# Two products of V and two of the next keys by turns, in place of four and four, in a cross-attention kernel on one core

## The chip, the core and the metric

The kernel runs on one NeuronCore of a Trainium2 chip. Its engines work side by side, each through its own instructions in order, and wait for one another by semaphores: TensorE (PE in the profile; PEld are its weight loads) multiplies matrices into PSUM, VectorE (DVE) and ScalarE (ACT) take results out of PSUM and compute on SBUF, GpSimd (POOL) computes on SBUF alone, and SyncE (SP) issues most DMAs. The metric is the device time of one execution in microseconds (us), as the median of several runs.

## What is computed

A cross attention in float32, for 16 batches of 100 queries of width 640, 8 heads of width 80, over 718 context rows of width 384. The last 4 of the 722 rows take a way of their own, whose result is added before the output projection. Cut to what matters:

```python
query = hidden_states @ Wq
keyt = enc @ Wk                       # enc: the first 718 rows, 384 wide
valt = enc @ Wv
hs = _mha(query, keyt, valt)          # 8 heads: softmax(q k^T / sqrt(80)) v
ca_hs1 = _mha(ca_q1, residual, residual)
ca_q2 = ca_hs1 @ Wq
ca_hs2 = _mha(ca_q2, ca @ Wk_ca, ca @ Wv_ca)   # ca: the last 4 rows
out = (hs + ca_hs2) @ Wout + b_out + residual
```

## The kernel before

One loop runs over the 16 batches (`b`, line 1218), with the order of every engine's instructions written out by hand: each engine takes its instructions in the order in which the program makes them. Each batch goes through the same stages. `scores` (three calls, L622) multiplies queries with keys for three pairs of key blocks and ScalarE copies the scores to the tiles `st[0]` to `st[2]`. VectorE takes the maximum (`larger`, L1252; the class `Maximum`). Then, while the maximum is being worked out, TensorE makes two things in small products: the values V of this batch (`vv`, class `Values`) and the keys of the next batch (`kk`, class `Keys`). After them come `last_keys` (L567), in some batches an output projection (`project_pair`, L1033) or the next queries (`queries`, L543), and at last the products of the exponentials with V (`a_ps`, L1432).

V and the keys are each made by a scheme of 15 products of sums of blocks, in place of 18 plain ones. `V_PLAN` lists for each product a PSUM bank (A to E), the form of the context and of the weights that it takes, and the block of the result into which the bank's content goes next. A bank isn't cleared between products: it goes on adding up, and after every product its content as it stands is taken out and added to one block (`Blocks.go`). So a product in a bank must wait until the content after the bank's previous product has been taken out. The first thing that reaches a block is a copy on ScalarE (L415), every later one an addition on VectorE (L413). `K_PLAN` is the same list for the keys, with two pairs of places exchanged.

In what follows v0 to v14 are the products of V in the order of `V_PLAN`, and k0 to k14 those of the keys in the order of `K_PLAN`. The banks that matter are:

| products | bank | block | taken out by |
|---|---|---|---|
| v3, k3 | A | (2, 0) | VectorE |
| v4, k4 | B | (2, 0) | VectorE |
| v5 | E (two PSUM buffers) | (1, 0) | VectorE, two additions |
| v6 | A | (1, 0) | VectorE |
| k5 | A | (1, 0) | VectorE |
| k6 | E | (1, 0) | VectorE |
| v7, k7 | B | (2, 1) | VectorE |
| v8, k10 | C | (0, 1) | ScalarE for v8, VectorE for k10 |
| v10, k12 | C | (2, 1) | VectorE |

A and B of V lie in a pair of banks each, A and B of the keys in a pool of two buffers (`psk`). C, D and E of both share one pool of two buffers (`ps1`) by turns: D of V takes both, then D of the keys one, then E of V both, E of the keys one, C of V both, C of the keys one. A product of V is two matmuls (two key blocks, L442) and one of the keys two (two chunks of the width, L473); the profile has two records for each matmul.

The function `both(n)` issues the next n products of V and then the next n of the keys, each with its removal. It is called in batches 1 to 14 (line 1311). Around the call that the change touches stand, in order: `top.go(3)`, `both(3)`, `now.scores2()`, `top.go(1)` (ScalarE spreads the maximum), `last.place()` (twenty small copies on ScalarE, L948), the touched call, `top.go()` (VectorE transposes the spread maximum into `over`, L704), `both(1)`, `now.softmax3()` (three small VectorE instructions, of which the last makes `p2`, L861), `now.values2()` (GpSimd's products and sums from `p2`, L875 and L882), two products of V and one of the keys, and then `subtract(0)` (L1240, VectorE takes `over` from the scores) and `exponential(0)` (ScalarE, L1248). The subtracts of the other two score tiles stand between the later products. In batches 3, 6, 8, 11 and 13 `last.load` has GpSimd add the bias to two tiles (L915) before `values2`, and the output of two blocks of rows is projected after `last_keys`.

Of the kernel before, what the change touches and what calls it, by code (L numbers as in the profile page):

```python
# [135 lines left out]
def kernel(  # L136
# [80 lines left out]
    def enc_tile(name):  # L217

        return inp.tile([P, NF, KT], F32, tag="enc", name=name)
# [14 lines left out]
    def load_rest(b, enc):  # L234
        if b == 1:
            room = hsT_tile("rest_1").rearrange("p c s -> p (c s)")
            rest = room[:, : len(A_REST) * KT].rearrange("p (i k) -> p i k", k=KT)
        else:
            rest = rest_tile(f"rest_{b}")
        for (u, c), i in A_REST.items():  # L240
            nc.sync.dma_start(
                out=rest[:, i], in_=enct[b][:, c, u * (KT - 1) : u * (KT - 1) + KT]
            )
        return enc[0], rest
# [347 lines left out]
    def last_keys(b, enc):  # L592
        banks = pair(f"kT_ps_{b}")
        return chunk_keys(
            HC - 1,
            [banks[:, k] for k in range(2)],
            [wk4[:, c] for c in range(CC)],
            enc,
        )
# [106 lines left out]
    def load_m(b):  # L706
        if b < 2:
            return lambda c: m_sb[c][:, b * HT : (b + 1) * HT]
        mb = small.tile([P, HC, HT], F32, tag="mb", name=f"mb_{b}", bufs=2)
        nc.sync.dma_start(  # L710
            out=mb, in_=m_d[:, :, b * HT : (b + 1) * HT].rearrange("c p n -> p c n")
        )
        return lambda c: mb[:, c]
# [504 lines left out]
    for b in range(B):  # L1218
# [5 lines left out]
        def loads():  # L1224

            if b == 0:
                nc.sync.dma_start(
                    out=wout_sb, in_=wout.rearrange("(c p) n -> p c n", p=P)
                )
            if b + 2 >= B:  # L1230
                return None, None
            x_next = xT_at[0] if b % 2 else load_x(p + 1)
            xT_at[0] = x_next
            return Second(b + 2, x_next), load_enc(b + 2)
# [4 lines left out]
        def subtract(i):  # L1239
            return nc.vector.tensor_tensor(  # L1240
                st[i],
                st[i],
                top.over[:KN].unsqueeze(1).to_broadcast([KN, 2, ROWS]),
                ALU.subtract,
            )

        def exponential(i):
            nc.scalar.activation(st[i], st[i], AF.Exp, scale=SCALE)  # L1248
# [59 lines left out]
        elif b + 1 < B:  # L1308
            vv = Values(b, e_in)

            def both(n):
                vv.go(n)
                kk.go(n)

            forms = [wout_sb[:, 2 * i : 2 * i + 2, k * (H // 2) : (k + 1) * (H // 2)]
                     for i in range(2) for k in range(2)]
            if b == 2:
                for o, left, right in (
                    (forms[1], forms[1], forms[0]),
                    (wout2[:, 0], forms[3], forms[1]),  # L1320
                    (wout2[:, 1], forms[2], wout2[:, 0]),
                ):
                    nc.gpsimd.tensor_tensor(o, left, right, ALU.subtract)
            elif last.b - 1 in PAIRS:
                nc.gpsimd.tensor_tensor(wout2[:, 0], wout2[:, 0], forms[0], ALU.add)
            second.scores1(seen)
            if b == 1:
                now.load()
            last.load()
            top.go(3)  # L1330
            both(3)
            now.scores2()
            top.go(1)
            if b > 1:
                last.place()
            both(4)
            top.go()
            both(1)
            now.softmax3()
            if b == 1:  # L1340
                nc.gpsimd.tensor_tensor(last.hs[:S], last.hs[:S], last.hs2, ALU.add)
            now.values2()
            if last.b in PAIRS:
                last.sums()
            vv.go(2)
            kk.go(1)
            subtract(0)
            exponential(0)
            vv.go(1)
            subtract(1)  # L1350
            vv.go(1)
            kk.go(2)
            exponential(1)
            vv.go(1)
            kk.go(2)
            both(1)
            both(1)
            if b == 1:
                for f in list(wv_there):
                    nc.scalar.copy(wv_sb[:, W_AT[f]], wv_there.pop(f))  # L1360
            second.load()
            if b == 1:
                nc.gpsimd.dma_start(out=bias, in_=bout[0].partition_broadcast(P))
            second_next, enc_next = loads()
            if b + 2 < B:
                m_next = load_m(b + 2)
            subtract(2)
            exponential(2)
            last_keys(b + 1, enc)
            if b + 2 < B:  # L1370
                enc_next = load_rest(b + 2, enc_next)
            if b == 1:
                last.transpose()
            if last.b in PAIRS:
                second.softmax1(3)
                last.project_pair()
                if last.b == max(PAIRS):
                    nc.sync.dma_start(
                        out=forms[1],
                        in_=wout[: 2 * P, H // 2 :].rearrange("(c p) n -> p c n", p=P),  # L1380
                    )
            second.softmax1()
        else:
            room = enc_tile("spare").rearrange("p f k -> p (f k)")
            spare.extend(room[:, i * H : (i + 1) * H] for i in range(2))
            last.transpose()
            vv = Values(b, e_in)
            last.load()
            mine.load()
            top.go(3)  # L1390
            vv.go(3)
            last.project_few(len(OC) - 2)
            now.scores2()
            top.go(1)
            vv.go(2)
            top.go()
            vv.go(3)
            now.softmax3()
            now.values2()
            vv.go(2)  # L1400
            subtract(0)
            exponential(0)
            vv.go(5)
            for i in (1, 2):
                subtract(i)
                exponential(i)
            last.project()
# [105 lines left out]
```

## Time and profile before

| | us |
|---|---|
| runs shown (3) | 942.48, 942.58, 943.21 |
| median | 942.58 |
| the profiled execution | 943.54 |
| its span, first to last instruction | 941.8 |
| TensorE matmuls busy | 930.6 (99%) |
| VectorE busy | 698.5 (74%) |
| GpSimd busy | 674.1 (72%) |
| ScalarE busy | 434.6 (46%) |
| 352 records of products of V in bank A, mean of one | 0.435 |
| 360 records of products of keys in bank A, mean of one | 0.369 |

The span is that of the one execution that the profiler recorded. Matmuls are pipelined: the records overlap, and a busy TensorE isn't a TensorE without gaps, so gaps are looked for in the distance from start to start. A row of the order of time gives the start and the length of a group in us, the engine, the line, the operation, output and inputs, the shapes, how many instructions are merged and, in brackets, idle time before them with what ended it. Idle time on an engine other than the one that sets the end costs nothing by itself. Batch 2 begins near 158 us, batch 3 near 206.6 us; its products of V and keys run from 215.5 to 244.8 us.

### The profile page before, as it was taken

What the parts mean: (1) busy time and instruction counts of PE and PEld (TensorE: products, weight loads), DVE (VectorE), ACT (ScalarE), POOL (GpSimd) and SP (SyncE); (2) the same over time, 40 slices, a digit from 0 to 9 for tenths busy, and PEclk for the clock granted to TensorE, in tenths of its full rate; (3) what the DMA queues carried; (4) which work ended last, traced back from release to release, by engine and by line L of the source; (5) the groups of instructions that cost most, each with busy time, mean ns of one, the idle gap of its engine ahead of it and who ended that gap; (6) DMA issues with size and microseconds to landing.
All of it is one profiled execution on the core that took longest, in us unless ns stands there. A gap on an engine that the chain in (4) does not pass through costs nothing.

```text
span 941.8 us, 25879 instructions
## 1 busy us (share of the span) xinstructions
PE 930.6 (99%) x11130; PEld 785.7 (83%) x11130; DVE 698.5 (74%) x1111; ACT 434.6 (46%) x836; POOL 674.1 (72%) x615
## 2 busy tenths in 40 slices
PE   9999999999999999999999999999999999999998
PEld 6998879797797878888798887988879888797866
DVE  3859794989739797695967859579783898838884
ACT  1235443736336363462635526264651736416341
POOL 5757998688937778497784968747895588945714
PEclk9999999999999999999999999999999999999999
DMA  8822022040300304031030310205030050310201
GB/s 258 280 71 71 23 79 62 5 149 2 101 31 20 106 1 130 3 93 61 14 117 3 111 43 29 75 2 151 4 96 34 2 152 2 101 45 2 80 18 41
DMA packets 49673, 62.82 MB, mean 67 GB/s; under 512 B 14072, under 2 KB 38200, under 8 KB 49560
## 3 DMA queue, kind: packets, MB, share of 16 engines
q1 hardware_dynamic: 45512, 51.49, 17.8%
q0 software_dynamic: 3024, 8.53, 2.9%
q8 instruction: 87, 1.43, 0.6%
q10 hardware_dynamic: 1024, 1.15, 0.4%
q14 instruction: 26, 0.21, 0.1%
HBM read 55.59 MB, written 5.57 MB: 65 GB/s over the span
## 4 chain that ended last, share of the span: by engine, by line
PE 85%; DVE 12%; issue 2%; ACT 1%; DMA 0%; POOL 0%; ACTq 0%; DVEq 0%
PE a_ps L1432 12%; PE s_ps L622 11%; PE kT_ps L567 8%; PE v_psA L442 8%; PE q_ps L543 7%; PE v_psB L442 7%; PE k_psA L473 6%; PE o_ps L1033 5%; PE k_psB L473 5%; PE v_psC L442 3%; DVE vs L413 3%; DVE st L1240 2%; PE k_psC L473 2%; DVE most L1252 2%; PE v_ps L383 2%
## 5 line engine op out<-in xcount | busy, mean ns | idle before, releaser
L783 POOL TENSOR_TENSOR e<-ca,g 100x800 f32<-100x800 f32 x64 | 99.4, 1563 | 133.4 <-DVE most L1252 124.2
L875 POOL TENSOR_TENSOR hs<-vb,p 100x640 f32<-100x640 f32 x64 | 119.8, 1881 | 53.1 <-DVE p L861 24.1
L508 POOL TENSOR_TENSOR enc<-enc 128x240 f32<-128x240 f32 x135 | 104.9, 786 | 20.0 <-DMA enc<-in_enct 12.9
L1432 PEld LDWEIGHTS a_ps<-vs,st 120*36 120x36 f32 (+3 forms) x3072 | 109.2, 125 | 5.7 <-issue 5.6
L1432 PE MATMUL a_ps<-vs,st 120*36 120x81 f32 (+3 forms) x3072 | 112.2, 233 | 0.7 <-issue 0.7
L442 PE MATMUL v_psA<-wv_sb,enc 128*120 128x320 f32 x352 | 110.0, 435 | 0.3
L1240 DVE TENSOR_TENSOR st<-st,over 120x1600 f32<-120x1600 f32 x48 | 107.1, 2234 | 0.0
L882 POOL TENSOR_TENSOR hs<-hs,hs 100x640 f32<-100x640 f32 x48 | 100.6, 2096 | 3.8
L622 PE MATMUL s_ps<-qp,kT 32*120 32x100 f32 x3072 | 98.3, 263 | 0.0
L622 PEld LDWEIGHTS s_ps<-qp,kT 32*120 32x120 f32 x3072 | 95.5, 179 | 1.7 <-issue 0.2
L639 ACT COPY st<-s_ps 120x800 f32<-120x800 f32 x64 | 49.7, 829 | 101.5 <-PE s_ps L622 101.5
L790 POOL TENSOR_TENSOR e<-e,e 100x800 f32<-100x800 f32 x48 | 90.5, 1886 | 3.8
L442 PE MATMUL v_psB<-wv_sb,enc 128*120 128x320 f32 x296 | 91.8, 433 | 0.0
L473 PE MATMUL k_psA<-enc,wk_sb 128*128 128x240 f32 x360 | 88.7, 369 | 3.0 <-DVE kT L413 2.2
L1248 ACT ACTIVATE st<-st 120x1600 f32<-120x1600 f32 x48 | 73.8, 1538 | 27.6 <-DVE st L1240 27.4
L1252 DVE TENSOR_TENSOR most<-most,st 120x800 f32<-120x800 f32 x64 | 68.7, 1074 | 23.3 <-ACT st L633 22.2
L473 PEld LDWEIGHTS k_psA<-enc,wk_sb 128*128 128x128 f32 x360 | 67.1, 190 | 22.3 <-issue 4.3
L442 PEld LDWEIGHTS v_psA<-wv_sb,enc 128*120 128x120 f32 x352 | 62.8, 183 | 24.4 <-DVE vs L413 2.9
L473 PE MATMUL k_psB<-enc,wk_sb 128*128 128x240 f32 x300 | 73.1, 366 | 0.3 <-DVE sm L858 0.3
L442 PEld LDWEIGHTS v_psB<-wv_sb,enc 128*120 128x120 f32 x296 | 54.1, 183 | 21.9 <-DVE vs L413 0.4
L1444 DVE RECIPROCAL rs<-a_ps 100x4 f32<-100x4 f32 x32 | 5.8, 180 | 86.0 <-PE a_ps L1432 86.0
L543 PE MATMUL q_ps<-xT,wq_sb 128*128 128x200 f32 x400 | 69.1, 333 | 0.0
(167 smaller groups left out, 1851.8 us busy)
## 6 DMA issues: line engine op xcount, KB each, us to landing
vb<-va_d POOLq DMA_DIRECT2D x32, 250.0 KB, 3.6
vb<-va_d SPq DMA_DIRECT2D x32, 250.0 KB
enc<-in_enct SPq DMA_DIRECT2D x30, 240.0 KB
enc<-in_enct SPq DMA_DIRECT2D x15, 360.0 KB
xT<-in_xt SPq DMA_DIRECT2D x8, 500.0 KB
rest<-in_enct SPq DMA_DIRECT2D x31, 120.0 KB
xn<-in_x SPq DMA_DIRECT2D x11, 320.0 KB
out<-xn SPq DMA_DIRECT2D x11, 320.0 KB
```

Of the source, the lines that this page charges most:

```text
L442: nc.tensor.matmul(at[0][j][:KN, : H // 2], a_form(self.enc, f)[:, j * KN : (j + 1) * KN], wv_there.get(f, wv_sb[:, W_AT[f]]), start=first ...
L473: nc.tensor.matmul(at[:, i * KT : (i + 1) * KT], wk_sb[:, W_AT[f], i], a_form(self.enc, f), start=(first and i == 0), stop=last, skip_grou ...
L508: nc.gpsimd.tensor_tensor(out, left, right, op)
L543: nc.tensor.matmul(q_ps[:, : 2 * S].rearrange("p (j s) -> p j s", j=2), wq_sb[:, c, n * P : (n + 1) * P], xT[:, :, c, :], start=(c == 0), ...
L622: nc.tensor.matmul(s_ps[r][:n, 256 * a + lo : 256 * a + hi], kT[rows, c, u, j * KN : (j + 1) * KN], rhs, start=(a == 0 and c == 0), stop=( ...
L783: first = nc.gpsimd.tensor_tensor(to, self.ca[:, t, :].unsqueeze(1).to_broadcast([S, NH, S]), g[:, :, t].unsqueeze(2).to_broadcast([S, NH, ...
L790: nc.gpsimd.tensor_tensor(e, e, to, ALU.add)
L875: first = nc.gpsimd.tensor_tensor(to, self.vb[t][:S].rearrange("p (h d) -> p h d", h=NH), p2[:, :, t].unsqueeze(2).to_broadcast([S, NH, D] ...
L882: nc.gpsimd.tensor_tensor(sums, sums, to, ALU.add)
L1240: return nc.vector.tensor_tensor(st[i], st[i], top.over[:KN].unsqueeze(1).to_broadcast([KN, 2, ROWS]), ALU.subtract,)
L1252: most_now = nc.vector.tensor_tensor(most[:KN], most[:KN], st[i][:, u], ALU.max)
L1432: nc.tensor.matmul(a_v[lo:hi, h % 4], st[i // 2][: KEYS[i], i % 2, h * S + lo : h * S + hi], block(i, h // 4)[: KEYS[i], h % 4], start=(i ...
```

## The change

One call becomes two, in batches 1 to 14:

```diff
             if b > 1:
                 last.place()
-            both(4)
+            both(2)
+            both(2)
             top.go()
             both(1)
             now.softmax3()
```

Before, the products come as v3, v4, v5, v6, k3, k4, k5, k6; after, as v3, v4, k3, k4, v5, v6, k5, k6. Every removal moves with its product, so VectorE's order becomes v3, v4, k3, k4, v5 (two additions), v6, k5, k6. Nothing else is changed.

## The prediction

> **What bounds the kernel now.** I read the page first, then the instructions of TensorE and of VectorE in order of time in two batches, then the same spots of all fourteen batches that run the changed line. The page:
>
> ```profile
> PE 930.6 (99%) x11130; PEld 785.7 (83%) x11130; DVE 698.5 (74%) x1111; ACT 434.6 (46%) x836; POOL 674.1 (72%) x615
> ...
> PE 85%; DVE 12%; issue 2%; ACT 1%; DMA 0%; POOL 0%; ACTq 0%; DVEq 0%
> ```
>
> The second line is the chain of work that ended last: 85% lies on TensorE and 12% on VectorE. So TensorE's work sets the end, and what can be won are the spots where it waits for VectorE. The order of time in batch 3 shows them (columns: start, length, engine, line, operation, tiles, count, idle time before and what ended it). TensorE:
>
> ```profile
> 223.35 1.24 PE L442 MATMUL v_psE<-wv_sb,enc 128*120 128x320 f32 x4
> 224.67 1.34 PE L442 MATMUL v_psA<-wv_sb,enc 128*120 128x320 f32 x4
> 225.85 0.97 PE L473 MATMUL k_psA<-enc,wk_sb 128*128 128x240 f32 x4
> 226.66 0.97 PE L473 MATMUL k_psB<-enc,wk_sb 128*128 128x240 f32 x4
> 227.98 1.05 PE L473 MATMUL k_psA<-enc,wk_sb 128*128 128x240 f32 x4 [0.35 <-DVE kT L413]
> 228.86 0.97 PE L473 MATMUL k_psE<-enc,wk_sb 128*128 128x240 f32 x4
> 229.67 1.24 PE L442 MATMUL v_psB<-wv_sb,enc 128*120 128x320 f32 x4
> ```
>
> Lengths overlap, so I go by starts. Undisturbed, a key product takes 0.81 us from start to start (225.85 to 226.66) and one of V 1.08 (the start of batch 2 has 166.88, 167.98, 169.06). Against that, v6 (the second v_psA) starts 0.25 late and its successor 0.10 more (the array fills again), and k5 (the second k_psA) 0.51 late, its successor 0.08 more: 0.94 us lost. VectorE in the same stretch:
>
> ```profile
> 223.81 0.81 DVE L413 TENSOR_TENSOR vs<-v_psA,vs 120x640 f32<-120x640 f32 x1
> 224.72 0.82 DVE L413 TENSOR_TENSOR vs<-v_psB,vs 120x640 f32<-120x640 f32 x1
> 225.46 0.88 DVE L413 TENSOR_TENSOR vs<-v_psE,vs 120x320 f32<-120x320 f32 x2
> 226.44 0.82 DVE L413 TENSOR_TENSOR vs<-v_psA,vs 120x640 f32<-120x640 f32 x1
> 227.19 0.65 DVE L413 TENSOR_TENSOR kT<-k_psA,kT 128x480 f32<-128x480 f32 x1
> ...
> 230.45 1.00 DVE L704 STREAM_TRANSPOSE over<-spread 128x800 f32<-128x800 f32 x1
> ...
> 233.09 0.97 DVE L861 TENSOR_TENSOR p<-e,sm 100x32 f32<-100x32 f32 x1
> ```
>
> Product v6 goes into bank A again and needs v3 (223.81 to 224.62) taken out. k5 likewise needs k3 taken out, which ends at 227.84. Only k4 stands between k3 and k5, 0.81 us, while a product's tail, the hop to VectorE and an addition of 0.66 take over 1.1. So k5 waits at least 0.35 (0.27 and 0.08) in every batch.
>
> **The same reading in all batches.** Early wait, v6 and k5 together: batch 1 0.99, batch 3 0.94, batch 5 0.96, batch 11 0.69, batch 13 0.77, batch 14 0.66, and 0.35 in each of 2, 4, 6, 7, 8, 9, 10, 12. Sum 7.81 us. A later wait stands at k12, the second k_psC, for the removal of k10: 0.60 in batch 1, 0.34 in eight others (2, 4, 5, 7, 9, 10, 12, 14), none in 3, 6, 8, 11, 13.
>
> **The change part by part.** No instruction is added or removed; 14 times v5, v6 trade places with k3, k4, with their eight matmuls each and five of VectorE's nine removals. No DMA and no ScalarE or GpSimd instruction is in the moved stretch, so the queues of SP and POOL are passed by nothing; ScalarE keeps its order, since all removals here are additions on VectorE.
>
> Switching between V and keys: now once per batch in this stretch, after it three times. The rows show k_psE to v_psB in 0.81 and v_psB to k_psB in 1.08, the undisturbed times, so it costs 0.
>
> v6 after v3: between them now v4, k3, k4, v5 instead of v4, v5. In batch 3 v6 would start at 221.20 + 1.08 + 1.08 + 0.81 + 0.81 + 1.08 = 226.05, and v3 is out at 224.62: no wait. k5 after k3: between them k4, v5, v6, 2.96 us in place of 0.81. k5 would start at 227.13; VectorE takes out v3 to 224.62, v4 to 225.55, k3 to 226.11: no wait. So the early wait goes in all batches, 7.81 us.
>
> Does VectorE follow? Its order is then v3, v4, k3, k4, v5 (two), v6, k5, k6. With the rows' lengths (an addition into what the one before wrote starts 0.10 after its end, any other 0.08 before): k4 226.87, v5 227.66, v6 228.59, k5 229.15, k6 229.92, and the transpose `over` starts at 229.83 instead of 230.45, 0.62 earlier. VectorE had idled 0.47 and 0.15 there. In batches with only the 0.35 wait, the removal of k6 follows TensorE's k6 by 0.04 as now, so VectorE moves by 0.35 with it.
>
> New waits: v5 opens E's two banks when D's are copied, which ScalarE has done by 221.96 in batch 3. k6 opens one of them again and needs v5 out: 227.27 against its start at 227.94, room of 0.67. In batch 2 the room is 1.2. It costs 0 here.
>
> Where the stall goes. After `over` comes p2 (L861), with both inputs in SBUF. It takes 0.19 us in batches 2, 4, 5, 7, 9, 10, 12, 14, but 0.97 in batch 3, where it ends with GpSimd's addition:
>
> ```profile
> 230.95 3.05 POOL L915 TENSOR_TENSOR xn<-xn,bias 128x640 f32<-128x640 f32 x2
> ```
>
> The two additions run to 234.00, p2 to 234.05, and only then the first subtract starts. The same holds in 6, 8, 11, 13 (L915) and in 1 (L790 to 127.40). There VectorE may arrive earlier and gets on no earlier, because GpSimd's chain began before the changed stretch. What TensorE gains is kept only up to k12, whose room is its start less the end of k10's removal: 0.28, 0.34, 0.33, 0.29, 0.29 in batches 3, 6, 8, 11, 13. Less 0.06 for the hop to TensorE (191.12 to 191.18 in batch 2) and 0.10 for the restart, 0.13 + 0.18 + 0.17 + 0.13 + 0.13 = 0.74. Batch 1 has no room and keeps 0.
>
> The open batches move as a whole: 2, 4, 7, 9, 10, 12 keep 0.35 each, 2.10; 14 keeps 0.66. Batch 5 keeps its 0.96 and more: its second subtract came 0.11 behind GpSimd's next product (353.125 against 353.015) and was held 1 us. The product stands behind p2 and moves 0.62, the subtract stands behind TensorE's v10 and moves 0.96, so now it goes first and the 0.33 at k12 goes too: 1.29.
>
> Sum: 2.10 + 0.66 + 1.29 + 0.74 = 4.79 us, of which nothing is lost later: the last exponential is covered by last_keys, 3.65 us, and by the 2.3 us that a_ps spends on the first two score tiles (in batch 2 it ends at 198.87 and is first used near 201.9), so the next batch starts earlier as a whole. The profiled execution took 943.54 (span 941.8), so 938.8 for it; it lies 0.96 above the median, and from the median 942.58 the forecast is 937.8.
>
> What is priced from no row is who wins when VectorE and GpSimd come at once. With the 0.62, p2 of batch 3 is ready at 232.47 and GpSimd's second addition starts at 232.45; batches 1, 11, 13 are as close. Bounds: p2 second, as summed; p2 first with the subtract straight after it, which frees the whole early wait there, 0.99 + 0.81 + 0.56 + 0.64 = 3.0 more; p2 first and then the subtract behind the addition, 1.55, which puts it 0.25 later than now and takes back 0.4 in each of these four, 1.6 less. I take p2 second, since it is nearest to the rows (0.11 late lost in batch 5).
>
> The Trainium skill, page "SBUF — State Buffer", section "SBUF: two separate sides", says that VectorE with two SBUF inputs and GpSimd take a shared port as an exclusive lock for a whole instruction, first come first; that is what p2's two lengths show. By it alone the earlier VectorE would be worth nothing wherever GpSimd started 0.02 before it, the 4.8 above, and 7.8 if it started 0.02 after; the page doesn't say who goes first at a tie.
>
> **The rivals.**
> - Everything early is kept, because p2 gets in between GpSimd's two additions: 4.8 + 3.0 = 7.8, so 934.8. For it: the margins are hundredths. Against: at present p2 is late in all four. 21%.
> - VectorE takes it back: its subtracts don't move in the eight open batches either, and the wait at k12 grows by what went early. Then 0.74 and perhaps half of batch 5 stay, about 1.4: 941.2. For it: k12 waits for VectorE already there. Against: VectorE's idle 0.47 and 0.15 before k5's and k6's removals show that TensorE paced it. 14%.
> - Slower: the place is k6, which needs E's bank, emptied 1.3 us later than now. It decides once VectorE is later than the sum by 0.67 (batch 3) or 1.2 (batch 2); the price is one for one beyond that. With each of the six additions from v3 to v5 0.35 longer than its row, 2.1 in all, the wait would be 1.4 in the five batches like 3 and 0.9 in the nine like 2, 15.1, less the 7.81, so 949.9. Against: additions in this very place hold 0.81 and 0.66 with GpSimd busy beside them. 5%.
> - The change doesn't do what it says: k5 waits for something else than k3's removal (a form written by GpSimd is also waited for). Then no difference, 942.6. 3%.
>
> **How the numbers follow.** The forecast, 3.4 to 6 us less (936.6 to 939.2), has 57%. The range 934.4 to 939.8 takes in the first rival. This kernel's measurement tells about 0.2%, 1.9 us, from no change: faster 0.57 + 0.21 + 0.04 of the second rival = 0.82, same 0.10 + 0.03 = 0.13, slower 0.05.
>
> **What would show it.** v5 to v6 and v6 to k5 1.08 from start to start, with no idle before either, in all 14 batches: the mechanism. `over` 0.6 earlier in batch 3 relative to the batch's start: VectorE follows. p2 still ending with L915, and a new wait of some 0.7 at k12 in batch 3, 0.3 in 6 and 8: the taking back; p2 at 0.19 there: the first rival. No wait at k12 in batch 5. A wait at k6 would speak for the slower case, and a k12 wait that grows in batch 2 for the second rival.

## The result and the profile after

| | before | after |
|---|---|---|
| median, us | 942.53 (6 runs, 942.06 to 943.53) | 937.99 (6 runs, 936.77 to 939.92) |
| the profiled execution, us | 943.54 | 936.77 |
| its span, us | 941.8 | 935.1 |

The ratio is 0.9952, with a 95% interval of 0.9939 to 0.9966: 4.5 us less, by an interval that lies wholly below 1. The profiled execution of after is the fastest of its six, so the two profiles stand further apart, 6.8 us, than the medians.

The page after, first the busy times, then the chain of work that ended last, then TensorE's group in `a_ps`:

```profile
PE 926.5 (99%) x11130; PEld 786.6 (84%) x11130; DVE 699.4 (75%) x1111; ACT 434.6 (46%) x836; POOL 674.8 (72%) x615
...
PE 86%; DVE 11%; issue 1%; DMA 1%; ACT 1%; POOL 0%; DVEq 0%
...
L1433 PE MATMUL a_ps<-vs,st 120*36 120x81 f32 (+3 forms) x3072 | 112.0, 233 | 0.0
```

The work is the same. The share of VectorE in the chain fell by a point. The last line had 0.7 us of idle time in the profile before and has none now, though nothing of it was changed; this comes back below.

The order of time of TensorE in batch 3 after, in the stretch that was shown before (columns as there):

```profile
220.05 1.24 PE L442 MATMUL v_psB<-wv_sb,enc 128*120 128x320 f32 x4
221.12 0.97 PE L473 MATMUL k_psA<-enc,wk_sb 128*128 128x240 f32 x4
221.94 0.97 PE L473 MATMUL k_psB<-enc,wk_sb 128*128 128x240 f32 x4
222.75 1.24 PE L442 MATMUL v_psE<-wv_sb,enc 128*120 128x320 f32 x4
223.82 1.24 PE L442 MATMUL v_psA<-wv_sb,enc 128*120 128x320 f32 x4
224.90 0.97 PE L473 MATMUL k_psA<-enc,wk_sb 128*128 128x240 f32 x4
225.71 0.97 PE L473 MATMUL k_psE<-enc,wk_sb 128*128 128x240 f32 x4
...
237.83 1.08 PE L473 MATMUL k_psC<-enc,wk_sb 128*128 128x240 f32 x4 [0.64 <-DVE kT L413]
```

From v4 to k6 every start follows the one before by 1.07 to 1.08 or 0.81 to 0.82: the waits at v6 and k5 are gone. At k12, the last line, there is now a wait that this batch didn't have. VectorE in the same batch, with GpSimd's additions of the bias below it:

```profile
226.41 0.65 DVE L413 TENSOR_TENSOR kT<-k_psA,kT 128x480 f32<-128x480 f32 x1
227.16 0.66 DVE L413 TENSOR_TENSOR kT<-k_psE,kT 128x480 f32<-128x480 f32 x1
227.74 1.00 DVE L704 STREAM_TRANSPOSE over<-spread 128x800 f32<-128x800 f32 x1
...
230.37 1.56 DVE L861 TENSOR_TENSOR p<-e,sm 100x32 f32<-100x32 f32 x1
231.85 1.81 DVE L1240 TENSOR_TENSOR st<-st,over 120x1600 f32<-120x1600 f32 x1
```

```profile
228.84 3.04 POOL L915 TENSOR_TENSOR xn<-xn,bias 128x640 f32<-128x640 f32 x2
```

p2 comes earlier and is only longer for it, 1.56 against 0.97: it still ends with GpSimd's second addition, at 231.9. What was lost at v6 and k5 before, 0.94, is lost at k12, 0.90 with the 0.10 at its successor.

Measured in every batch, from the first matmul of `y_ps` to the first of last_keys, and beside it what the prediction's sum kept for it:

| batch | before | after | less | forecast |
|---|---|---|---|---|
| 1 | 30.93 | 29.54 | 1.40 | 0 |
| 2, 4, 7, 9, 10, 12 (each) | 30.03 to 30.04 | 29.69 to 29.70 | 0.33 to 0.34 | 0.35 |
| 3 | 30.29 | 30.27 | 0.02 | 0.13 |
| 5 | 30.63 | 29.69 | 0.94 | 1.29 |
| 6, 8 | 29.71, 29.70 | 29.53, 29.52 | 0.18, 0.19 | 0.18, 0.17 |
| 11 | 30.04 | 30.11 | -0.06 | 0.13 |
| 13 | 30.12 | 30.12 | 0.00 | 0.13 |
| 14 | 30.34 | 29.73 | 0.61 | 0.66 |
| sum | | | 5.29 | 4.79 |

The other 1.46 us between the two profiles lie outside the products. 0.83 is a hold in the middle of `a_ps`, at 322.1 in the execution before (in the last quarter of batch 4) and not in this one, in which TensorE waited for nothing that the profile shows; 0.49 lies ahead of batch 1's products. Such holds come and go in kernels with the change and without it: the execution profiled of the kernel e3 below, which has four and four, has two in `a_ps`, 0.59 and 1.17 us, and lies 2.3 us above that kernel's median. So they aren't counted to the change; where they stand is in the last section.

### The profile page after: what moved, and what is told of

It is laid out like the page before. It is cut to its first block, busy times and chain, and to the rows that moved or that the text cites. A ratio compares the mean times of both kernels' runs of the same rounds, so it can differ in the third digit from the quotient of the medians.

```text
span 935.1 us, 25893 instructions
## 1 busy us (share of the span) xinstructions
PE 926.5 (99%) x11130; PEld 786.6 (84%) x11130; DVE 699.4 (75%) x1111; ACT 434.6 (46%) x836; POOL 674.8 (72%) x615
## 3 DMA queue, kind: packets, MB, share of 16 engines
q10 hardware_dynamic: 1024, 1.15, 0.4%
## 4 chain that ended last, share of the span: by engine, by line
PE 86%; DVE 11%; issue 1%; DMA 1%; ACT 1%; POOL 0%; DVEq 0%
PE a_ps L1433 12%; PE s_ps L622 12%; PE v_psA L442 8%; PE kT_ps L567 8%; PE q_ps L543 7%; PE v_psB L442 7%; PE k_psA L473 6%; PE o_ps L1033 5%; PE k_psB L473 5%; PE v_psC L442 3%; DVE st L1240 3%; DVE vs L413 2%; PE k_psC L473 2%; DVE kT L413 2%; DVE most L1252 2%; PE y_ps L748 2%
## 5 line engine op out<-in xcount | busy, mean ns | idle before, releaser
L1252 DVE TENSOR_TENSOR most<-most,st 120x800 f32<-120x800 f32 x64 | 68.4, 1068 | 22.4 <-ACT st L633 21.3
L948 ACT COPY hsT<-turned_hs 32x160 f32<-32x160 f32 (+7 forms) x244 | 67.7, 278 | 3.0
```

What stands on the lines that cost most here:

```text
L1252: most_now = nc.vector.tensor_tensor(most[:KN], most[:KN], st[i][:, u], ALU.max)
```

## The experiments

Each kernel was compared with the kernel before on the same chip. "Products" is the stretch of the table above. 29.36 us is its length without any wait at a product.

**The changed kernel again** (`e1_after_again`, no edit).

> The changed kernel once more, to see which of its spots differ between two profiled executions. Theory (GpSimd and VectorE meet within hundredths of a us at p2 of batches 1, 3, 11, 13): the early wait at v6 and k5 is 0 in all 14 batches again; from the first key product to last_keys the open batches 2, 4, 7, 9, 10, 12 again take 0.33 to 0.34 us less than before; batches 1, 3, 11, 13 may come out differently, by up to 1 us each. Rival (nothing in it is a race, the differences between executions lie outside the products): these four come out as in the first profile, 1.40, 0.02, -0.06 and 0.00 less. Median 938.0, within 0.8.

937.34 us (936.23 to 937.54), ratio 0.9942 [0.993, 0.9954]. No wait at v6 or k5. The open batches kept 0.33 to 0.35 again, batches 6 and 8 0.19 and 0.18. Batch 1 kept 1.41, batch 3 0.36, batch 5 1.27, and 11 and 13 lost 0.23 and 0.16. So the open batches repeat to hundredths and 3, 5, 11 and 13, where VectorE meets GpSimd, don't. The theory holds in that, but not in the place of the race: p2 came second in 3, 11 and 13 again (1.57 to 1.59 long), batch 1 came out as in the first profile, and batch 5, which the theory hadn't named, differed by 0.33. What moved is how late in the stretch the two engines come to p2; this is taken up below.

**Seven switches instead of three** (`e2_by_ones`).

```diff
-            both(2)
-            both(2)
+            for _ in range(4):
+                both(1)
```

> One product of V and one of the keys by turns, four times, in place of two and two: seven switches between V and keys instead of three. Theory (a switch costs nothing, and any order with over 1.2 us between two products of one bank has no wait): no wait at v6 or k5, open batches as in the changed kernel within 0.05 us, median 938.0 within 1.0; VectorE's additions into one block no longer follow each other directly, so `over` may come up to 0.4 earlier in batches 3, 11, 13. Rival (switching weights and output banks costs TensorE time, hidden in the changed kernel's gain): four more switches in 14 batches, at 0.05 us or more each, give at least 2.8 us more, 940.8 or slower.

937.10 us (936.90 to 937.68), ratio 0.9943 [0.993, 0.9955]. No wait at v6 or k5, and the open batches take 29.69 to 29.70, as in the changed kernel. A switch between V and keys costs nothing that can be seen. In batches 1, 3, 11 and 13 the products fell to 29.33 to 29.36, since `over` comes as early as in the open batches (15.05 us after the start of the stretch, against 15.3 to 15.5). Part of that was given back in the projection of batch 3 and nearly all in those of 11 and 13: the shift against the kernel before, after which the next batch starts, is 0.4, 0.7 and 0.7 us smaller than the products' gain of 0.93, 0.68 and 0.76. In 11 and 13 TensorE waits there for GpSimd's sums (L1014).

**Bank A kept apart without interleaving** (`e3_key_banks`), on the kernel before:

```diff
-K_PLAN = [V_PLAN[k] for k in (0, 1, 2, 3, 4, 6, 5, 7, 9, 11, 8, 12, 10, 13, 14)]
+K_PLAN = [V_PLAN[k] for k in (0, 1, 2, 3, 4, 5, 6, 7, 9, 11, 8, 12, 10, 13, 14)]
```

> The kernel before, with four and four, but with k5 and k6 exchanged in the list of the keys: k3 (bank A), k4 (B), E, A. Between k3 and the next key product of bank A lie 1.62 us instead of 0.81. Theory (k5's wait is the wait for bank A): no wait at the fifth and sixth key product; the wait at v6 in batches 3, 5, 11, 13 (0.1 to 0.35) stays; open batches take 0.3 less than before, batches 6 and 8 0.18 less, so 3 to 4.5 us less in all, 938 to 939.5. Rival (what the changed kernel wins comes from spreading the products of V and keys, and so VectorE's work): within 1 us of before, 941.5 or more.

In `K_PLAN` places 5 and 6 stand exchanged against `V_PLAN`, and places 8 to 12 in another order; the edit undoes the exchange. 937.32 us (936.96 to 939.66), ratio 0.9943 [0.9929, 0.9956], somewhat faster than expected. TensorE in batch 2:

```profile
174.93 1.24 PE L442 MATMUL v_psA<-wv_sb,enc 128*120 128x320 f32 x4
176.00 0.97 PE L473 MATMUL k_psA<-enc,wk_sb 128*128 128x240 f32 x4
176.81 0.97 PE L473 MATMUL k_psB<-enc,wk_sb 128*128 128x240 f32 x4
177.62 0.97 PE L473 MATMUL k_psE<-enc,wk_sb 128*128 128x240 f32 x4
178.43 0.97 PE L473 MATMUL k_psA<-enc,wk_sb 128*128 128x240 f32 x4
```

With E between the two products of A every key product starts 0.81 after the one before, and the open batches take 29.69 to 29.70, the same as with the change. The wait at v6 stayed in batches 1 and 3, at 0.41 and 0.46 with its successor; in 5 it went, and in 11 and 13 0.08 was left. So the change's gain is the bank's, not that of spreading the work: four and four with two list places exchanged reaches the time of the changed kernel on the same chip (937.34 in e1).

**The two products of A side by side** (`e11_a_after_a`), on the kernel before: the same list with k5 straight behind k3.

```diff
-K_PLAN = [V_PLAN[k] for k in (0, 1, 2, 3, 4, 6, 5, 7, 9, 11, 8, 12, 10, 13, 14)]
+K_PLAN = [V_PLAN[k] for k in (0, 1, 2, 3, 6, 4, 5, 7, 9, 11, 8, 12, 10, 13, 14)]
```

> The kernel before, with k5 (bank A) put straight behind k3 (bank A), ahead of k4: nothing lies between the two. Theory (the wait is the time from the end of a product to the end of its removal and back, 1.16 us from the next product's earliest start, less what lies between): the wait at the second of them rises by the 0.81 of the product taken away, to 1.16 in the open batches; the later waits stay within 0.1; 0.81 in 14 batches is 11.3 us, 952 to 954, a little less where the wait at k12 in batches 3, 6, 8, 11, 13 had room. Rival (the early wait was VectorE's backlog at that time, whichever bank comes): the wait stays near 0.35, 942.5 within 1.5.

956.87 us (956.60 to 956.96), ratio 1.0149 [1.0135, 1.0163]. TensorE and VectorE in batch 2:

```profile
178.69 0.97 PE L473 MATMUL k_psA<-enc,wk_sb 128*128 128x240 f32 x4
180.57 1.05 PE L473 MATMUL k_psA<-enc,wk_sb 128*128 128x240 f32 x4 [0.91 <-DVE kT L413]
```

```profile
179.77 0.66 DVE L413 TENSOR_TENSOR kT<-k_psA,kT 128x480 f32<-128x480 f32 x1
181.66 0.66 DVE L413 TENSOR_TENSOR kT<-k_psA,kT 128x480 f32<-128x480 f32 x1 [1.23 <-PE k_psA L473]
```

From start to start 1.88 in place of 0.81, a wait of 1.08, and 0.07 at the next product: 1.15, the 0.35 plus the 0.81 that was taken away. VectorE is idle for 1.23 meanwhile, so it was no backlog. The open batches take 0.81 longer, as the theory has it. The whole is 2.9 us above the upper end of what it said. In batches 6 and 8 the products take 1.14 and 1.13 longer, in 3, 11 and 13 1.34, 1.20 and 1.15: p2 now comes after GpSimd's additions, takes 0.19, and the wait at k12 appears as in the open batches. Batch 0 makes its keys by the same list and takes 1.34 longer, which the expectation left out.

**The bias later** (`e4_bias_late`): GpSimd's additions leave `last.load` and stand behind `values2`.

```diff
                     nc.sync.dma_start(out=to, in_=rows[:, cols])
-                    nc.gpsimd.tensor_tensor(to, to, bias[at : at + n, cols], ALU.add)
+                    self.biased.append((to, bias[at : at + n, cols]))
...
             now.values2()
+            last.add_bias()
             if last.b in PAIRS:
                 last.sums()
```

> The changed kernel with GpSimd's additions of the bias (L915) moved behind its products and sums from p2 (L875, L882). Theory (in batches 3, 6, 8, 11, 13 p2 is held by these additions, and that is why little of the early wait is kept there): p2 takes 0.19 in all five, in 3, 11, 13 the first subtract starts over 1 us earlier and 0.5 to 0.9 us more is kept in each, in 6 and 8 the products take what they take in the open batches, 0.2 more than in the changed kernel; in all 1 to 2.3 us less, 935.7 to 937. Rival (VectorE is late in 3, 11, 13 by itself, and the hold at p2 costs nothing): 938.0 within 0.5.

945.09 us (943.29 to 947.26), ratio 1.0027 [1.0016, 1.0037]: slower than the kernel before, against the expectation. In the products the theory held in the main. p2 takes 0.19 in all five batches, 3, 11 and 13 take 29.76, 29.76 and 29.36 (0.51, 0.35 and 0.75 less than in the changed kernel, where 0.5 to 0.9 was expected), and 6 and 8 take 29.70. But in each of the five the projection then came late. TensorE after last_keys of batch 3, and GpSimd:

```profile
246.09 2.86 PE L1039 MATMUL o_ps<-wout_sb,hsT 128*128 128x320 f32 x10
249.78 2.42 PE L1039 MATMUL o_ps<-wout,hsT 128*128 128x320 f32 x8 [0.82 <-POOL hsT L1020]
```

```profile
245.19 3.04 POOL L920 TENSOR_TENSOR xn<-xn,bias 128x640 f32<-128x640 f32 x2
248.18 0.74 POOL L1020 TENSOR_TENSOR sum<-hsT 128x256 f32<-128x256 f32 x1
249.00 0.72 POOL L1020 TENSOR_TENSOR hsT<-sum,hsT 128x256 f32<-128x256 f32 x1
```

The sums for the projection (L1020 here, L1014 before) stand behind the moved 3 us on GpSimd, and TensorE waits for them. Against the products' gain, 1.4 us was lost in each of batches 3, 6, 8 and 11 and 2.1 in 13, 7.7 in all. The time that GpSimd is given at p2 it needs at the projection.

**The bias earlier** (`e7_bias_early`): the rows are loaded a batch ahead, and the additions stand in front of `second.scores1`.

```diff
+            if b > 1:
+                last.add_bias()
             second.scores1(seen)
             if b == 1:
                 now.load()
-            last.load()
...
             second.load()
+            if b + 2 < B:
+                mine.load()
```

> The changed kernel with the rows of x loaded a batch earlier and GpSimd's additions of the bias (L915) done ahead of its products for the next batch's first softmax, where GpSimd waits for VectorE anyway, in place of behind its products from p2. Theory (p2 is held by these additions; moved behind, they made the output projection wait for GpSimd's sums, 1.4 us in each of five batches): p2 takes 0.19 in batches 3, 6, 8, 11, 13, the products take 29.4 to 29.8 in 3, 11, 13 and 29.70 in 6 and 8, and the projection doesn't wait for the sums; 1 to 2.4 us less than the changed kernel, 935.5 to 937. Rival (those additions have to cost something wherever they stand: GpSimd's chain begins up to 3.1 us later in 3, 11, 13 and p2 meets its last product instead): 938.0 or more.

938.02 us (937.07 to 938.54), ratio 0.9948 [0.9935, 0.9961]: no better than the changed kernel, as the rival said, though not by its mechanism. p2 takes 0.19 in the five batches and the projection doesn't wait. But batches 3 and 13 take 30.81 and 30.45, with waits at v6 and k5. VectorE there, with GpSimd's additions:

```profile
214.88 3.84 DVE L1258 TENSOR_TENSOR most<-most,st 120x800 f32<-120x800 f32 x2
```

```profile
213.34 4.54 POOL L920 TENSOR_TENSOR xn<-xn,bias 128x640 f32<-128x640 f32 x2
```

The maximum of two tiles in SBUF (L1252 in the kernel before) takes 2.01 for two where GpSimd is idle, and 3.84 here, in turns with the additions. So VectorE reaches v3's removal 1.8 us later in batch 3, and the early wait is back. There is a new one too: in batches 3, 11 and 13 k6 starts 0.21 to 0.26 late, and the loading of its weights waits for VectorE's removal of v5, which is the wait for E's bank of the prediction's slower case.

**k12 later** (`e6_k12_later`), on the changed kernel:

```diff
             exponential(1)
             vv.go(1)
-            kk.go(2)
-            both(1)
+            kk.go(1)
+            vv.go(1)
+            kk.go(2)
             both(1)
```

> The changed kernel with v13 between k11 and k12 (v12, k11, v13, k12, k13 in place of v12, k11, k12, v13, k13), 1.08 us more between k10 and k12. Theory (what is not kept, and what is left to win, stands at k12, which waits for k10's removal behind the second subtract): no wait at k12; the products from the first to last_keys take 29.36 to 29.45 us in all of batches 2 to 14, which is their length without any wait; sum over the batches 5 to 6 us less than the changed kernel, 932 to 933. Rival (VectorE as a whole is too slow there, and k12 is only the first to show it): the wait comes back at k13 or v14, under 1 us is won, 937 or more.

934.15 us (933.48 to 934.50), ratio 0.9909 [0.9896, 0.9922]. TensorE at the end of batch 2's products:

```profile
188.47 0.97 PE L473 MATMUL k_psA<-enc,wk_sb 128*128 128x240 f32 x4
189.28 1.24 PE L442 MATMUL v_psB<-wv_sb,enc 128*120 128x320 f32 x4
190.36 0.97 PE L473 MATMUL k_psC<-enc,wk_sb 128*128 128x240 f32 x4
191.17 0.97 PE L473 MATMUL k_psB<-enc,wk_sb 128*128 128x240 f32 x4
```

k12 (the k_psC) starts 1.08 after v13, without a wait. The products take 29.36 in all batches but 3 and 11 (29.54 and 29.75, with a wait at v13). The expectation was 932 to 933, and 934.15 is short of it by some 1.5 us: the projections of 3 and 11 give back 0.3 each, and the profiled execution has two holds in `a_ps`, 0.42 and 0.39. So k12 was the one place where the open batches' remaining time was.

**k12 later alone** (`e10_k12_alone`), the same edit on the kernel before.

> The kernel before, with four and four, and v13 ahead of k12 as the only edit. Theory (the early wait for bank A and the late wait at k12 are two waits, and each can be taken away by itself): the early wait stays at 0.35 in the open batches, k12's goes; the products take 29.70 in 2, 4, 7, 9, 10, 12 in place of 30.03; 0.34 in eight batches and 0.6 in batch 1 make 3.3 less, 938.9 to 939.7. Rival (both are one lateness of VectorE, and what is taken away late comes back early or at the next product): under 1 us less, 941.6 or more.

940.30 us (939.85 to 941.40), ratio 0.9976 [0.9967, 0.9985]. The open batches take 29.70 with the early wait at 0.34 as before; the two waits are separate. 0.33 was won in each of them. In the profiled execution batches 11 and 13 took 0.42 longer, with VectorE late at v6, which is part of why only 2.6 us came of 3.3.

**All three, and without the bias** (`e8_all_three`: by ones, k12 later, bias early; `e9_ones_k12`: without the last).

> The changed kernel with three edits together: by ones in place of two and two, v13 ahead of k12, and the bias added early. Theory: no wait in any product of batches 2 to 14, 29.36 each, 5.5 us less than the changed kernel, 932 to 933, and no more than the edit at k12 alone by over 1. Rival (the edits take the same wait away from different sides, and the early bias costs GpSimd what it saves VectorE): slower than the edit at k12 alone.

> By ones in place of two and two, and v13 ahead of k12; the bias as in the changed kernel. Theory: as the edit at k12 alone, but with VectorE earlier in batches 3, 11, 13, so that the products take 29.36 there too: 932 to 933, within 0.7 of the edit at k12 alone. Rival (the hold at p2 costs time also without a wait at k12, further on): 1 us or more slower than the kernel with all three.

934.42 us (932.12 to 937.67), ratio 0.9913 [0.9898, 0.9928], and 934.53 us (933.62 to 935.31), ratio 0.9913 [0.9901, 0.9926]. In both the products take 29.33 to 29.37 in all 14 batches, so nothing is left to win at a product. Neither is faster than k12 later alone on top of the change. With the bias early the profiled execution has the shortest span of all, 930.4 us, and the projection gives nothing back; its six runs differ by 5.5 us, and what sets them apart was not found, since one execution of each kernel was profiled.

The fastest version by the median is the changed kernel with k12 later, 934.15 us: 8.6 us less than the kernel before on its chip (942.76). The change alone saved 4.5 and 5.2 us on the two other chips where it ran, so v13 ahead of k12 adds some 3.4 to 4.1 to it.

## Why the prediction was right, point by point

**The early wait.** The reading that v6 and k5 wait for their bank, and that the change takes both away in all 14 batches, is what the trace after shows, and e3 and e11 show the reason by themselves: a second product between k3 and k5 removes the wait, taking away the one that was there adds 0.81.

**The switches cost nothing.** Shown with three by the starts in batch 3 and with seven by e2.

**The open batches move as a whole.** 0.33 to 0.34 against 0.35 forecast, in all six, and 0.33 to 0.35 in e1, e2, e3, e4 and e7. Batch 14 had 0.61 against 0.66.

**p2 takes back what 3, 6, 8, 11 and 13 win.** Shown by the longer p2 of the trace after and by e4 and e7, where p2 has its 0.19 once the additions are elsewhere. In 6 and 8 the size was right to 0.02. In 3, 11 and 13 the forecast was 0.13 each and 0.02, -0.06 and 0.00 came. There GpSimd's additions begin later in the stretch than in the profile before, by 0.11, 0.19 and 0.14 us (in batch 3 16.59 after its start, against 16.48), and VectorE's first removal with them; as much less was kept. In e1 they begin 0.25 earlier in 3 and 0.37 and 0.30 later in 11 and 13, and 0.36, -0.23 and -0.16 came. So the account is right, and the term that was mis-sized is the room at k12: it was read from one execution, and the start of the additions isn't the same in another. That is also why `over` came 0.49 earlier in batch 3 and not 0.62. The wait at k12, which the signs put at 0.7 in batch 3 and 0.3 in 6 and 8, was 0.90, and 0.16 and 0.15; by the prediction's own sum (what is won less what is kept) it would have been 0.81 and 0.17.

**Batch 1.** Here the step that failed was the tie: the prediction took p2 second, and it was first. VectorE and GpSimd in batch 1 after:

```profile
125.03 0.19 DVE L861 TENSOR_TENSOR p<-e,sm 100x32 f32<-100x32 f32 x1
125.14 1.82 DVE L1240 TENSOR_TENSOR st<-st,over 120x1600 f32<-120x1600 f32 x1
```

```profile
125.05 3.66 POOL L790 TENSOR_TENSOR e<-e,e 100x800 f32<-100x800 f32 x1
```

p2 starts 0.02 us ahead, takes 0.19, and the subtract straight after it goes first too; GpSimd's sum, 1.88 in the profile before, takes 3.66. That is the upper bound of the unknown cost, and it was worth 1.40 us where 0 was forecast, more than the 0.99 of the early wait that the bound allowed, since most of k12's wait went with it. The Trainium skill's rule of the exclusive lock (page "SBUF — State Buffer", section "SBUF: two separate sides") agrees with p2 and the sum: the loser waits for the whole of the other's instruction. That the subtract, which came 0.09 after the sum, went ahead of it as well is not what "first come" would give.

**Batch 5.** The early 0.96 came, by 0.94, but not the 0.33 at k12: in this execution VectorE wasn't late at v6, so p2, and GpSimd's products behind it, moved by the same 0.94 as the subtract (18.95 to 18.01 and 21.75 to 20.81 us after the start of the stretch), and the subtract kept its place behind the second product. The step that failed is the 0.62, which the prediction took over from batch 3. In e1's profile VectorE was late by 0.25 and the subtract went first: 1.27 less, the step as forecast.

**The sum.** 5.29 in the profiles' products against 4.79; the errors of batch 1 (+1.40) and of 3, 5, 11 and 13 (-0.78) partly cancel. In the medians the change is worth 4.54, so the forecast of 937.8 lies 0.2 from the 937.99 measured. That closeness is partly luck, since the six runs before differ by 1.47 us and the six after by 3.15.

**The rivals.** VectorE taking all back is ruled out by the open batches. The slower case, a wait at k6 for E's bank, didn't appear: no wait at k6 in the trace after, nor in e2, and the room there was 0.54 in batch 3 and 1.30 in batch 2 (0.67 and 1.2 forecast). It is a real limit all the same, as e7 shows, where VectorE is 1.8 us later. The first rival, everything early kept, happened in one of its four batches. That k5 waits for something else than k3's removal is ruled out by e3 and e11. One count of the prediction is wrong without a consequence: on each side four matmuls trade places, which are eight records, not eight matmuls.

## What to carry to other kernels

Where products go on adding up in a bank that is taken out after each, count the time from the end of a product to the end of its removal and back, 1.16 us here, and put as much other work between two products of a bank; in the orders tried here it didn't matter which work it was or in how many pieces. A wait taken away is only kept as far as the next place where the same engines meet, so look for that place before and repair both: the early and the late wait were worth 4.5 to 5.2 and 2.6 us by themselves, and 8.6 together. An engine with a quarter of its time idle can still have no free place: GpSimd's 3 us of additions cost as much or more at each of the two other spots where they were put.

## What the runs showed of the hardware

VectorE and GpSimd held each other up for whole instructions where both read two SBUF operands, and hundredths of a us decided it: in the kernel after, p2 took 0.19 in batch 1, with GpSimd's sum 0.02 behind it, and 1.56 in batch 3, where GpSimd's second addition began 0.03 ahead of it. The maximum of two score tiles took 3.84 in place of 2.01 beside two additions. VectorE's removals from PSUM, which have one operand in SBUF, took 0.61 to 0.66 for 128x480 and 0.78 to 0.83 for 120x640 in every profile, GpSimd busy or not.

Single holds of 0.4 to 1.2 us in `a_ps`, in which TensorE waits for nothing that the profile shows, came in six of the twelve profiled executions, and always at one of two places: records 164 to 170 of the 192 of `a_ps` in batch 4 (six times) or in batch 12 (twice). The traces hold the packets of a queue of the kind `instruction` (q8), which moves 16 KB at a time. In all eight holds the held matmul starts 1.2 to 1.5 us after the end of such a transfer, and that end lies between 0.9 us ahead of record 161 and 0.1 behind it; in the sixteen other passes through these two places it lies 0.9 to 2.1 us ahead, and at most 0.13 us is lost. So the holds look like TensorE waiting for its own instructions, but no run varied this, and the cause is not shown. The six profiled executions without a hold are each the fastest of their kernel's runs; of the six with one or two, three are the slowest (before, e3, e6) and one the fastest (e8). The holds are larger than most of the single steps that were forecast; the rows of the open batches repeated to 0.01 us where the times of whole executions didn't repeat to 1.
